# Attention scores of a Pre-LN block with a mixture of experts: PSUM tiles of two banks in place of one

## The chip, the cores and the metric

The kernel runs on one core of a Trainium2 chip. The metric is the device time of one execution in microseconds (us). The time before is 618.14 us, the median of three runs (616.91, 624.91 and 618.14).

## The reference

One transformer block over x of shape 8 x 512 x 128, everything in float32: layer norm, causal attention with 16 heads of width 8, a residual sum, a second layer norm, and 8 experts of width 512, of which each token uses the two that its gate likes best.

```
x = x + attn(layernorm(x))          # q, k, v of 16 heads x 8; scores causal; softmax; @ Wo + bo
x = x + ffn(layernorm(x))           # 8 experts, top 2 by softmax(x @ gate_w.T), relu, weighted sum
```

## The kernel before, in words

The work is laid out by batch (b, 8 of them), and inside a batch by groups of four heads (g, 4 per batch). Every engine has a fixed order of instructions. It is written by hand as several generators ("lanes"): each yields the point of the schedule, counted in batches, at which its next piece is to stand, and the lane with the smallest point goes next. The lanes that matter here:

- `project` (L393) makes layer norm, q and k of a batch ahead of time, splits them into three bf16 parts and sends them through DRAM into the packed buffers q2 and k2, where a head's three parts lie on the rows of one matmul.
- `shifts` (L555) finds each query's largest score. For each pair of heads it goes through three units (`S_UNITS`): TensorE writes blocks of scores into PSUM tiles named s (L593, L598), and VectorE takes a maximum over each tile into pm (L612). After two pairs it reduces pm to nm, splits it into two bf16 parts (L618 to L629), transposes them on TensorE, copies them on ScalarE (L562) and sends them by two DMAs on SyncE's queue (POOL's for batch 0) into two rows of q2 (L568). So a later matmul subtracts the maximum by itself. The transpose and the DMAs are popped from a list, one entry after each unit. This lane runs 0.55 of a batch (`LEAD`) ahead of the next.
- `attend` (L638) computes the scores once more, transposed and with the maximum subtracted, into PSUM tiles named st (L740, L745). ScalarE takes the exponential of each into pt (L750). TensorE multiplies pt with v into po (`product`, L657, matmuls at L667). Every unit ends with `go_on` (L645), which pops one waiting product and one late step (the division at L682, the transpose of the output, the projection).
- `route`, `dispatch` and `experts` run beside the attention of later batches: gate, choice, scatter of the tokens to DRAM, tiles of 128 tokens per expert (ph at L1238, the relu at L1245 or L1247, py at L1097), a store, and a weighted sum at the end (`sums`). POOL's scatters and stores also wait for the last exponential ahead of them (`in_order`). About 490 us into the span the attention is over and only expert work is left.

PSUM has 8 banks of 512 float32 columns. One, ps_o, holds po; three, ps_mm, serve everything else; four, the pool ps_sc, serve s and st in rotation, one bank per tile, and the ph of the late expert tiles. Which free buffer of a pool a tile gets is settled when the program is built.

A unit names, for each bank, the heads and blocks that lie in it. The first and second units of a pair fill two banks (one bank per head), the third fills one bank with blocks of both heads. So a group of four heads has ten s banks and ten st banks, each with its own maximum (L612) or its own exponential (L750) over 512 columns. Nothing needs a bank's neighbour: the maximum over one bank can run while TensorE fills the next.

In the program's order an s unit and an st unit alternate: s unit, st unit with a product or a late step behind it, s unit, and so on; in a group there are six of each.

Of the kernel before, what the change touches and what calls it, by code (L numbers as in the profile page):

```python
# [9 lines left out]
F32 = mybir.dt.float32  # L10
# [8 lines left out]
P = 128  # L19
# [7 lines left out]
def preln_attn_moe(ctx: ExitStack, tc: tile.TileContext, x, wq, wk, wv, wo, bo,  # L27
# [52 lines left out]
    WARM = (40, 75, 4)  # L80
    XB = 3

    S_UNITS = (
        (((0, 3, 0),), ((1, 3, 0),)),
        (((0, 0, 0), (0, 2, P)), ((1, 0, 0), (1, 2, P))),
        (((0, 1, 0), (1, 1, 2 * P)),),
    )
    T_UNITS = (
        (((0, 0, 0),), ((1, 0, 0),)),
        (((0, 1, 0), (0, 3, 3 * P)), ((1, 1, 0), (1, 3, 3 * P))),  # L90
        (((0, 2, 0), (1, 2, 2 * P)),),
    )


    GROUPS = ((0, 1, 2, 3, 4, 5, 6), (7,))
# [24 lines left out]
    work = ctx.enter_context(tc.tile_pool(name="work", bufs=2))  # L120
    small = ctx.enter_context(tc.tile_pool(name="small", bufs=2))
    slots = ctx.enter_context(tc.tile_pool(name="slots", bufs=1, space=DRAM))
    ps_sc = ctx.enter_context(tc.tile_pool(name="ps_sc", bufs=4, space=PSUM))
    ps_mm = ctx.enter_context(tc.tile_pool(name="ps_mm", bufs=3, space=PSUM))
    ps_o = ctx.enter_context(tc.tile_pool(name="ps_o", bufs=1, space=PSUM))

# [428 lines left out]
    def shifts():  # L555
# [18 lines left out]
        for b in range(B):  # L574
            for g in range(G):
                t0 = b - LEAD + g / G + (0.1 if b == 0 < g else 0.0)
                yield t0
                assert b in packed
                q2, k2 = q2_buf[b % 2], k2_buf[b % 2]

                pm = pm_buf[g % 2].rearrange("p (n u) t k -> p u n (t k)", u=2)
                for pr in range(2):
                    n = 2 * g + pr
                    for i, unit in enumerate(S_UNITS):
                        yield t0 + (3 * pr + i) / 24
                        for v, bank in enumerate(unit):
                            ps = ps_sc.tile(
                                [P, T], F32, tag="sc", name=f"s_{b}_{n}_{i}_{v}"
                            )
                            for u, t, at in bank:  # L590
                                h, q = 2 * n + u, ts(t, P)
                                if t > 0:
                                    nc.tensor.matmul(  # L593
                                        ps[:, at : at + t * P], lhsT=q2[:KS, h, q],
                                        rhs=k2[:KS, h, : t * P],
                                        start=(at == 0), stop=True, skip_group_check=True,
                                    )
                                nc.tensor.matmul(  # L598
                                    ps[:, at + t * P : at + (t + 1) * P],
                                    lhsT=q2[:, h, q], rhs=k2[:, h, q],  # L600
                                    start=(at + t == 0), stop=True, skip_group_check=True,
                                )
                            blocks = ps.rearrange("p (a q) -> p a q", q=P)
                            if i == 0:
                                top, src = pm[:, v, pr, 12:13], ps
                            elif i == 1:
                                top, src = pm[:, v, pr, 3:7], blocks
                            else:
                                top, src = pm[:, :, pr, 8], ps.rearrange(
                                    "p (u k) -> p u k", u=2  # L610
                                )
                            nc.vector.tensor_reduce(top, src, AX.X, ALU.max)  # L612
                        if t0 + (3 * pr + i) / 24 < 0:
                            keep_warm(WARM[2], f"{g}_{pr}_{i}")
                        if late:
                            late.pop(0)()
                nm = small.tile([P, HG * NT], F32, tag="nm", name=f"nm_{b}_{g}")
                nc.vector.tensor_reduce(  # L618
                    nm, pm_buf[g % 2].rearrange("p h t k -> p (h t) k"), AX.X, ALU.max,
                    negate=True,  # L620
                )
                nh = nh_buf[g % 2]
                nm = nm.rearrange("p (h o a) -> p h o a", o=2, a=2)
                hi, lo = (
                    nh[:, ts(l, HG * NT)].rearrange("p (h a o) -> p h o a", a=2, o=2)
                    for l in range(2)
                )
                V.tensor_copy(hi, nm)
                V.tensor_tensor(lo, nm, hi, ALU.subtract)  # L629
                if b > 0:  # L630
                    late.append(lambda: None)
                late.append(lambda b=b, g=g, nh=nh: transposed(b, g, nh))
# [5 lines left out]
    def attend():  # L638
# [11 lines left out]
            for step in ready:  # L650
                step()

        def at_cols(pt, unit, u, at, W):
            v = u if len(unit) == 2 else 0
            return pt[:, v, at : at + W]

        def product(b, g, pts, unit, first, last):  # L657
            va = va_buf[b % 2]
            for j in sorted({j for bank in unit for _, j, _ in bank}):
                W = T - j * P  # L660
                for pr in range(2):
                    for bank in unit:
                        for u, i, at in bank:
                            if i != j:
                                continue
                            h = 2 * pr + u
                            nc.tensor.matmul(  # L667
                                po[32 * h : 32 * h + VC, j * P :],
                                lhsT=va[:, j, HG * g + h, :],
                                rhs=at_cols(pts[pr], unit, u, at, W),  # L670
                                start=(first and j == 0), stop=(last and j == 2),
                            )
            if last:
                ob = work.tile([P, T], F32, tag="ob", name=f"ob_{b}_{g}", bufs=1)
                nc.scalar.copy(ob, po)
                if b < B - 1:
                    late.append(lambda: None)
                late.append(lambda: divide(b, ob, g))
                if g == G - 1:
                    added.add(b)  # L680
# [40 lines left out]
        for b in range(B):  # L721
            for g in range(G):
                yield b + g / G
                assert (b, g, 2) in shifted
                q2, k2 = q2_buf[b % 2], k2_buf[b % 2]
                for i, unit in enumerate(T_UNITS):
                    pts = []
                    for pr in range(2):
                        yield b + g / G + (2 * i + pr + 0.5) / 24
                        n = 2 * g + pr  # L730
                        pt = work.tile(
                            [P, 2, T], F32, tag="pt", name=f"pt_{b}_{n}_{i}", bufs=6
                        )
                        for v, bank in enumerate(unit):
                            ps = ps_sc.tile(
                                [P, T], F32, tag="sc", name=f"st_{b}_{n}_{i}_{v}"
                            )
                            for u, j, at in bank:
                                h, k = 2 * n + u, ts(j, P)
                                nc.tensor.matmul(  # L740
                                    ps[:, at : at + P], lhsT=k2[:, h, k], rhs=q2[:, h, k],
                                    start=(at == 0), stop=True, skip_group_check=True,
                                )
                                if j < NT - 1:
                                    nc.tensor.matmul(  # L745
                                        ps[:, at + P : at + T - j * P],
                                        lhsT=k2[:KO, h, k], rhs=q2[:KO, h, (j + 1) * P :],
                                        start=False, stop=True, skip_group_check=True,
                                    )
                            last_exp[0] = nc.scalar.activation(pt[:, v, :], ps, AF.Exp, scale=SCALE)  # L750
                        pts.append(pt)
                        go_on()
                    products.append(lambda b=b, g=g, pts=pts, unit=unit, i=i: product(
                        b, g, pts, unit, i == 0, i == 2))
                attended.add((b, g))
        t = B
        while products or late:
            t += 0.5 / 24
            yield t
            go_on()  # L760

# [272 lines left out]
    def experts():  # L1034
# [192 lines left out]
        for n, (s, i) in enumerate(tiles):  # L1227
            first, m = quad(s, i)
            yield when(s, i + 1)
            if after(s, i):  # L1230
                ph = ps_sc.tile([P, T], F32, tag="sc", name=f"ph_{s}_{i}")
                hT = work.tile([P, 2, T], F32, tag="pt", name=f"hT_{s}_{i}", bufs=6)
                hT = hT[:, 0, :].rearrange("p (c t) -> p c t", c=FC)
            else:
# [140 lines left out]
```

## Time and profile before

| | |
|---|---|
| median of three runs | 618.14 us |
| the profiled execution, its own time | 610.58 us |
| its span from first to last instruction | 608.9 us |
| mean granted clock of TensorE | 0.949 |
| VectorE: maximum over 128x512 (L612) | 320 of 683 ns, 206.4 us |
| ScalarE: exponential over 128x512 (L750) | 320 of 599 ns, 177.6 us |
| attention of batch 1, 4, 6 (from its first st to the next batch's) | 49.2, 58.0, 56.3 us |

In the page, each engine has a line with its busy time; a busy TensorE is not one at its peak, since the ends of matmuls are modelled. In the groups, a row shows line, engine, operation and tiles, the count, the busy time with the mean of one, and the idle time of the engine just before such instructions with the one that ended it. In the timeline each row has its start in us, its length, engine, line and what it writes from what; brackets hold the idle time before it.

### The profile page before, as it was taken

What the parts mean: (1) busy time and instruction counts of PE and PEld (TensorE: products, weight loads), DVE (VectorE), ACT (ScalarE), POOL (GpSimd) and SP (SyncE); (2) the same over time, 40 slices, a digit from 0 to 9 for tenths busy, and PEclk for the clock granted to TensorE, in tenths of its full rate; (3) what the DMA queues carried; (4) which work ended last, traced back from release to release, by engine and by line L of the source; (5) the groups of instructions that cost most, each with busy time, mean ns of one, the idle gap of its engine ahead of it and who ended that gap; (6) DMA issues with size and microseconds to landing.
All of it is one profiled execution on the core that took longest, in us unless ns stands there. A gap on an engine that the chain in (4) does not pass through costs nothing.

```text
span 608.9 us, 14141 instructions
## 1 busy us (share of the span) xinstructions
PE 526.4 (86%) x4804; PEld 381.0 (63%) x4804; DVE 435.1 (71%) x1407; ACT 312.2 (51%) x685; POOL 188.4 (31%) x220
## 2 busy tenths in 40 slices
PE   7879998988877888889899999998999889889980
PEld 4655455555444554656566677775667579789970
DVE  6787688678986777787888786898684256323594
ACT  2646566655564574546455565564464434244530
POOL 3032200203413230162243213514314534655441
PEclk9989799999987899999899999999899999899995
DMA  2658187286379436521662486232135588667793
GB/s 56 177 135 169 44 215 164 67 186 169 80 152 166 116 96 166 135 60 44 156 145 60 119 173 170 71 87 88 49 81 145 163 252 234 181 196 240 218 315 111
DMA packets 68762, 86.07 MB, mean 141 GB/s; under 512 B 11540, under 2 KB 50748, under 8 KB 66652
## 3 DMA queue, kind: packets, MB, share of 16 engines
q1 hardware_dynamic: 63300, 75.10, 49.0%
q0 software_dynamic: 4800, 9.41, 4.6%
q8 instruction: 39, 0.64, 0.5%
q10 hardware_dynamic: 592, 0.66, 0.3%
q14 instruction: 31, 0.25, 0.2%
HBM read 61.34 MB, written 26.16 MB: 144 GB/s over the span
## 4 chain that ended last, share of the span: by engine, by line
PE 48%; DVE 24%; ACT 9%; DMA 7%; issue 7%; SPq 2%; another core or an unknown queue 1%; POOL 1%; ACTq 0%; DVEq 0%; POOLq 0%
DVE pm L612 11%; PE po L667 10%; PE py L1097 7%; PE ph L1238 6%; ACT pt L750 5%; PE st L745 4%; PE s L593 4%; PE st L740 4%; PE s L598 3%; PE oqp L687 3%; DMA q<-nmT 2%; DMA q<-ys 2%; PE pq L444 2%; DVE x L1316 2%; ACT hT L1245 2%
## 5 line engine op out<-in xcount | busy, mean ns | idle before, releaser
L750 ACT ACTIVATE pt<-st 128x512 f32<-128x512 f32 x320 | 177.6, 599 | 133.3 <-PE st L740 55.5
L612 DVE TENSOR_REDUCE pm<-s 128x1 f32<-128x512 f32 (+2 forms) x320 | 206.4, 683 | 31.2 <-PE s L598 25.7
L1135 POOL DMA_INDIRECT ys<-yo,to x78 | 75.5, 968 | 139.3 <-ACT pt L750 21.6
L593 PE MATMUL s<-k,q 72*128 72x384 bf16 (+2 forms) x384 | 94.6, 282 | 19.5 <-DVE pm L612 9.2
L740 PE MATMUL st<-q,k 128*128 128x128 bf16 x512 | 94.0, 225 | 12.6 <-DMA q<-nmT 4.6
L598 PE MATMUL s<-k,q 128*128 128x128 bf16 x512 | 94.9, 225 | 7.3 <-ACT pt L750 4.9
L667 PE MATMUL po<-pt,va 128*9 128x512 f32 (+3 forms) x1024 | 99.5, 460 | 1.1 <-ACT pt L750 1.0
L1003 POOL DMA_INDIRECT xs<-xn_f,slot x64 | 62.2, 972 | 116.8 <-ACT pt L750 85.1
L745 PE MATMUL st<-q,k 74*128 74x256 bf16 (+2 forms) x384 | 94.6, 284 | 0.0
L1097 PE MATMUL py<-w_sb,hT 128*128 x624 | 87.1, 281 | 7.7 <-issue 4.5
L1097 PEld LDWEIGHTS py<-w_sb,hT 128*128 128x128 f32 x624 | 77.7, 194 | 10.0 <-issue 5.5
L598 PEld LDWEIGHTS <-q 128*128 128x128 bf16 x512 | 51.6, 101 | 30.9 <-issue 27.8
L593 PEld LDWEIGHTS <-q 72*128 72x128 bf16 x384 | 38.2, 101 | 37.7 <-issue 31.3
L740 PEld LDWEIGHTS <-k 128*128 128x128 bf16 x512 | 52.5, 103 | 12.1 <-issue 5.2
L745 PEld LDWEIGHTS <-k 74*128 74x128 bf16 x384 | 38.4, 100 | 19.6 <-issue 14.3
L667 PEld LDWEIGHTS po<-pt,va 128*9 128x9 f32 x1024 | 21.3, 90 | 35.5 <-issue 24.0
L1238 PE MATMUL ph<-xgT,wt 128*128 128x128 f32 x288 | 40.1, 282 | 0.7 <-ACT xgT L1199 0.6
L1238 PEld LDWEIGHTS ph<-xgT,wt 128*128 128x128 f32 x288 | 35.0, 192 | 5.4 <-PE st L740 1.7
L1245 ACT ACTIVATE hT<-ph,q 128x128 f32<-128x128 f32 x72 | 20.9, 371 | 27.9 <-PE ph L1238 14.8
L690 DVE RECIPROCAL rd<-oqp 128x16 f32<-128x16 f32 x32 | 8.2, 255 | 36.9 <-PE oqp L687 31.6
L687 PEld LDWEIGHTS oqp<-ident,ob 128*128 128x128 f32 x128 | 14.4, 148 | 29.7 <-issue 28.3
L454 POOL TENSOR_TENSOR part<-rest,part 128x512 bf16<-128x512 f32 x14 | 16.1, 1158 | 50.0 <-ACT part L453 21.8
(170 smaller groups left out, 717.2 us busy)
## 6 DMA issues: line engine op xcount, KB each, us to landing
wt<-wrows SPq DMA_DIRECT2D x36, 322.0 KB
k<-kparts SPq DMA_DIRECT2D x42, 192.0 KB
q<-wrows SPq DMA_DIRECT2D x24, 322.0 KB
k<-wrows SPq DMA_DIRECT2D x18, 322.0 KB
q<-qparts SPq DMA_DIRECT2D x30, 192.0 KB
q<-ys SPq DMA_DIRECT2D x15, 256.0 KB
k<-xs SPq DMA_DIRECT2D x42, 65.0 KB
qparts<-part SPq DMA_DIRECT2D x14, 192.0 KB
```

The lines of the kernel that those rows point to most:

```text
L593: nc.tensor.matmul(ps[:, at : at + t * P], lhsT=q2[:KS, h, q], rhs=k2[:KS, h, : t * P], start=(at == 0), stop=True, skip_group_check=True,)
L598: nc.tensor.matmul(ps[:, at + t * P : at + (t + 1) * P], lhsT=q2[:, h, q], rhs=k2[:, h, q], start=(at + t == 0), stop=True, skip_group_che ...
L612: nc.vector.tensor_reduce(top, src, AX.X, ALU.max)
L667: nc.tensor.matmul(po[32 * h : 32 * h + VC, j * P :], lhsT=va[:, j, HG * g + h, :], rhs=at_cols(pts[pr], unit, u, at, W), start=(first and ...
L740: nc.tensor.matmul(ps[:, at : at + P], lhsT=k2[:, h, k], rhs=q2[:, h, k], start=(at == 0), stop=True, skip_group_check=True,)
L745: nc.tensor.matmul(ps[:, at + P : at + T - j * P], lhsT=k2[:KO, h, k], rhs=q2[:KO, h, (j + 1) * P :], start=False, stop=True, skip_group_c ...
L750: last_exp[0] = nc.scalar.activation(pt[:, v, :], ps, AF.Exp, scale=SCALE)
L1003: ins = nc.gpsimd.indirect_dma_start(out=xs[k], out_offset=bass.IndirectOffsetOnAxis(ap=slot[b][:, j * NT + i : j * NT + i + 1], axis=0), ...
L1097: nc.tensor.matmul(py, lhsT=hT[:, c, :], rhs=w2_sb[:, bass.ds(at[s, i] + c * E * D, D)], start=(c == 0), stop=(c == FC - 1),)
L1135: ins = nc.gpsimd.indirect_dma_start(out=ys[k], out_offset=bass.IndirectOffsetOnAxis(ap=to[s, first][:, i - first : i - first + 1], axis=0 ...
L1238: nc.tensor.matmul(ph[:, ts(c, P)], lhsT=wt[s, i][:, ts(c, P)], rhs=turned[s, first][:, ts(i - first, P)], start=True, stop=True,)
L1245: nc.scalar.activation(hT[:, c, :], ph[:, ts(c, P)], AF.Relu, bias=bias)
```

## The change

The pool ps_sc gets two buffers of two banks (1024 columns) in place of four of one. The units are drawn anew, for a group of four heads at once: five s units and five st units, each of which fills both banks of one tile. One maximum (L612 before) reads all 1024 columns, and so does one exponential (L750 before). The matmuls into the tiles are the same ones; their number, shapes and sums do not change. The points of the schedule within a group go in steps of 1/20 of a batch in place of 1/24, so lists that pop one entry per unit pop five per group in place of six. A product is queued after the second, the fourth and the fifth st unit. The late ph tiles take half of a two-bank tile each, in turn.

```diff
     S_UNITS = (
-        (((0, 3, 0),), ((1, 3, 0),)),
-        (((0, 0, 0), (0, 2, P)), ((1, 0, 0), (1, 2, P))),
-        (((0, 1, 0), (1, 1, 2 * P)),),
+        (((0, 0, 3, 0),), ((0, 1, 3, 0),)),
+        (((0, 0, 0, 0), (0, 0, 2, P)), ((0, 1, 0, 0), (0, 1, 2, P))),
+        (((1, 0, 3, 0),), ((1, 1, 3, 0),)),
+        (((1, 0, 0, 0), (1, 0, 2, P)), ((1, 1, 0, 0), (1, 1, 2, P))),
+        (((0, 0, 1, 0), (0, 1, 1, 2 * P)), ((1, 0, 1, 0), (1, 1, 1, 2 * P))),
     )
     T_UNITS = (
-        (((0, 0, 0),), ((1, 0, 0),)),
-        (((0, 1, 0), (0, 3, 3 * P)), ((1, 1, 0), (1, 3, 3 * P))),
-        (((0, 2, 0), (1, 2, 2 * P)),),
+        (((0, 0, 0, 0),), ((0, 1, 0, 0),)),
+        (((1, 0, 0, 0),), ((1, 1, 0, 0),)),
+        (((0, 0, 1, 0), (0, 0, 3, 3 * P)), ((0, 1, 1, 0), (0, 1, 3, 3 * P))),
+        (((1, 0, 1, 0), (1, 0, 3, 3 * P)), ((1, 1, 1, 0), (1, 1, 3, 3 * P))),
+        (((0, 0, 2, 0), (0, 1, 2, 2 * P)), ((1, 0, 2, 0), (1, 1, 2, 2 * P))),
     )
+    UNITS = len(S_UNITS)
...
-    ps_sc = ctx.enter_context(tc.tile_pool(name="ps_sc", bufs=4, space=PSUM))
+    ps_sc = ctx.enter_context(tc.tile_pool(name="ps_sc", bufs=2, space=PSUM))
...
-                pm = pm_buf[g % 2].rearrange("p (n u) t k -> p u n (t k)", u=2)
-                for pr in range(2):
-                    n = 2 * g + pr
-                    for i, unit in enumerate(S_UNITS):
-                        yield t0 + (3 * pr + i) / 24
-                        for v, bank in enumerate(unit):
-                            ps = ps_sc.tile(
-                                [P, T], F32, tag="sc", name=f"s_{b}_{n}_{i}_{v}"
+                pm = pm_buf[g % 2].rearrange("p (n u) t k -> p n u (t k)", u=2)
+                for i, unit in enumerate(S_UNITS):
+                    yield t0 + i / (UNITS * G)
+                    ps = ps_sc.tile([P, 2, T], F32, tag="sc", name=f"s_{b}_{g}_{i}")
+                    for v, bank in enumerate(unit):
...
-                            if i == 0:
-                                top, src = pm[:, v, pr, 12:13], ps
-                            elif i == 1:
-                                top, src = pm[:, v, pr, 3:7], blocks
-                            else:
-                                top, src = pm[:, :, pr, 8], ps.rearrange(
-                                    "p (u k) -> p u k", u=2
-                                )
-                            nc.vector.tensor_reduce(top, src, AX.X, ALU.max)
...
+                    pr, _, t, _ = unit[0][0]
+                    if t == 3:
+                        top, src = pm[:, pr, :, 12], ps
+                    elif t == 0:
+                        top, src = pm[:, pr, :, 3:7], ps.rearrange("p v (a q) -> p v a q", q=P)
+                    else:
+                        top, src = pm[:, :, :, 8], ps.rearrange("p v (u k) -> p v u k", u=2)
+                    nc.vector.tensor_reduce(top, src, AX.X, ALU.max)
...
+                pts = []
                 for i, unit in enumerate(T_UNITS):
-                    pts = []
-                    for pr in range(2):
-                        yield b + g / G + (2 * i + pr + 0.5) / 24
...
+                    yield b + g / G + (i + 0.5) / (UNITS * G)
+                    pt = work.tile([P, 2, T], F32, tag="pt", name=f"pt_{b}_{g}_{i}", bufs=6)
+                    ps = ps_sc.tile([P, 2, T], F32, tag="sc", name=f"st_{b}_{g}_{i}")
...
-                            last_exp[0] = nc.scalar.activation(pt[:, v, :], ps, AF.Exp, scale=SCALE)
-                        pts.append(pt)
-                        go_on()
-                    products.append(lambda b=b, g=g, pts=pts, unit=unit, i=i: product(
-                        b, g, pts, unit, i == 0, i == 2))
...
+                    last_exp[0] = nc.scalar.activation(pt, ps, AF.Exp, scale=SCALE)
+                    pts.append((pt, unit))
+                    go_on()
+                    if i % 2 == 1 or i == UNITS - 1:
+                        products.append(lambda b=b, g=g, pts=pts, i=i: product(
+                            b, g, pts, i == 1, i == UNITS - 1))
+                        pts = []
...
-                ph = ps_sc.tile([P, T], F32, tag="sc", name=f"ph_{s}_{i}")
+                if sum(after(*a) for a in tiles[:n]) % 2 == 0:
+                    two = ps_sc.tile([P, 2, T], F32, tag="sc", name=f"ph_{s}_{i}")
+                    ph = two[:, 0, :]
+                else:
+                    ph = two[:, 1, :]
```

## The prediction

> **What bounds the kernel now.** I read the page first (busy time, chain, groups), then busy time by stretches, then the timeline of one stretch.
>
> ```profile
> PE 526.4 (86%) x4804; PEld 381.0 (63%) x4804; DVE 435.1 (71%) x1407; ACT 312.2 (51%) x685; POOL 188.4 (31%) x220
> ...
> PE 48%; DVE 24%; ACT 9%; DMA 7%; issue 7%; SPq 2%; another core or an unknown queue 1%; POOL 1%; ACTq 0%; DVEq 0%; POOLq 0%
> DVE pm L612 11%; PE po L667 10%; PE py L1097 7%; PE ph L1238 6%; ACT pt L750 5%; PE st L745 4%; PE s L593 4%; PE st L740 4%; PE s L598 3%; PE oqp L687 3%; DMA q<-nmT 2%; DMA q<-ys 2%; PE pq L444 2%; DVE x L1316 2%; ACT hT L1245 2%
> ...
> L750 ACT ACTIVATE pt<-st 128x512 f32<-128x512 f32 x320 | 177.6, 599 | 133.3 <-PE st L740 55.5
> L612 DVE TENSOR_REDUCE pm<-s 128x1 f32<-128x512 f32 (+2 forms) x320 | 206.4, 683 | 31.2 <-PE s L598 25.7
> L593 PE MATMUL s<-k,q 72*128 72x384 bf16 (+2 forms) x384 | 94.6, 282 | 19.5 <-DVE pm L612 9.2
> ```
>
> TensorE carries the chain for half the span, VectorE for a quarter; ScalarE is half idle. The largest single entry of the chain is the maximum. The last row shows that TensorE's score matmuls already wait for it.
>
> ```profile
> 100.00:160.00 60.00, 51.21 (x487) 31.38 (x486) 49.49 (x143) 35.17 (x69) 14.20 (x14) 0.97 0.58 142
> 340.00:400.00 60.00, 58.01 (x579) 42.83 (x578) 45.79 (x145) 33.53 (x77) 19.52 (x20) 1.00 0.56 138
> ```
>
> The columns are length, then busy time of PE, PEld, DVE, ACT and POOL, the granted clock, DMA share and GB/s. In early batches VectorE (49.5 of 60) and TensorE share the load; once expert tiles run, TensorE is full (58.0 of 60), so what holds TensorE back costs time there.
>
> ```profile
> 206.81 0.22 PE L740 MATMUL st<-q,k 128*128 128x128 bf16 x1
> 206.87 0.22 PE L745 MATMUL st<-q,k 74*128 74x128 bf16 x1
> ...
> 207.04 0.22 PE L598 MATMUL s<-k,q 128*128 128x128 bf16 x1
> ...
> 207.40 1.28 DVE L612 TENSOR_REDUCE pm<-s 128x1 f32<-128x512 f32 x2
> ...
> 209.02 1.25 DVE L612 TENSOR_REDUCE pm<-s 128x4 f32<-128x512 f32 x2
> ...
> 211.09 0.69 DVE L612 TENSOR_REDUCE pm<-s 128x2 f32<-128x512 f32 x1
> ...
> 211.83 0.32 PE L593 MATMUL s<-k,q 72*128 72x384 bf16 x1 [0.68 <-DVE pm L612]
> ...
> 212.22 0.28 PE L740 MATMUL st<-q,k 128*128 128x128 bf16 x2
> 212.33 0.27 PE L745 MATMUL st<-q,k 74*128 74x256 bf16 x1
> 212.44 0.22 PE L740 MATMUL st<-q,k 128*128 128x128 bf16 x1
> 212.53 1.08 ACT L750 ACTIVATE pt<-st 128x512 f32<-128x512 f32 x2 [0.65 <-PE st L740]
> ```
>
> At 207.04 TensorE begins the next s unit although the maxima over the last one run only from 207.40 to 208.68: the four banks let it run ahead. At 211.83 it can't, and idles 0.68 us until the maximum of 211.09 ends. At 212.53 the exponential starts on its first bank while the second is being filled (the last matmul starts at 212.44).
>
> **The change part by part.** The sum is made against the profiled execution: 610.58 us (span 608.9, 1.7 around it). The median of the runs is 7.6 above it; I add that at the end.
>
> Durations. A 128-column bf16 matmul follows the last after 0.056 us (206.81 to 206.87). 1024 columns of scores are eight such, 0.45 us at most. A reader starts 0.03 us after the modelled end of the last matmul (212.28 + 0.22 = 212.50, read at 212.53), so 0.21 us after TensorE is free to go on. The waiting matmul starts 0.05 us after the read ends (211.78 to 211.83). Two maxima in a row take 1.28 us, one 0.684, so a second 512 columns costs 0.60 in a separate instruction. The short reduction over 64 columns (L618) takes 0.220 us: (684 - 220)/448 is 1.036 ns a column. One maximum over 1024 thus takes 0.684 + 0.53 = 1.22 us. For ScalarE, the bf16 copy over 2048 columns (L248) takes 1893 ns and the exponential over 512 takes 599: 0.842 ns a column, so 599 + 431 = 1.03 us against 1.086 for two.
>
> 1. VectorE's saving. 128 pairs save 0.06 each (8 us); 32 times two lone maxima (1.37) become one (1.22) (5 us): 13 us of 206. The maximum is on the chain for 65 of its 206 us, 31%: -4 us. Bounds: 0 and -13.
>
> [...]
>
> 2. ScalarE's saving by the same count: 128 x 0.06 + 32 x (1.20 - 1.03) = 13 us; 30 of its 178 us are on the chain, 17%: -2 us. Bounds: 0 and -13.
>
> 3. TensorE's waits. With two tiles, a fill must wait until the whole tile is read: 0.21 + 1.22 + 0.05 = 1.48 us after an s fill, 0.21 + 1.03 + 0.05 = 1.29 after an st fill. The instruction order of the changed program says which tile each fill takes and what TensorE has to do since that tile's last fill. Example (batch 4, group 2): s_2, st_1 (0.44 of work), s_3: 1.04 us short. I counted this for all 318 fills with row durations (0.22 for a 128x128 float32 product, 0.87, 0.66, 0.44 and 0.23 for four heads' po at 512 to 128 columns). 58 s fills after s are short, by 32 us in all; 35 st after st, 22 us; 24 s fills that take the tile of the st fill just before, 18 us; 13 st after s, 7 us: together 79 us. The same count for before, by bank, a unit's longer wait alone, gives 44 us. The rows of before name only about 30 us of such waits of TensorE (9.2 for L593 on the maximum, and L598, L740 and the waits on exponentials beside it), 0.68 of the count, since one wait shortens the next. So (79 - 44) x 0.68 = +24 us. Bounds: where only TensorE-led stretches count (69%), +16. From above: in the trace 109 s fills start before the maxima over the s unit ahead have ended, by 82 us together, and 45 st fills by 20 us; if all of that is lost in TensorE-led stretches, 102 x 0.69 = +70. I take +24, since it is counted on the order that will run. Behind a waiting fill stand, on TensorE's queue, the st fill, the product and the expert matmuls; ScalarE and POOL's stores wait for those.
>
> 4. VectorE's waits. Where VectorE is the limit, an s fill can start only after its maximum ends: 0.05 + 0.45 + 0.21 = 0.7 us until the next can start. Before, the second bank's maximum covered that. Now other VectorE work must: in the changed order 22 pairs of maxima have nothing between them, 43 have less than 0.7; the shortfall is 24 us in all. Times 31%: +7 us. Bounds: 0 (TensorE leads anyway) and +24.
>
> 5. The rows of the maximum. The transposed maximum's two DMAs go out after the third of five units in place of the third of six; the copy, the transpose and the two DMAs on SyncE's queue each come later by 2/20 + 1/4 - (2/24 + 1/4) = 1/60 batch, 0.9 us of 56. Three st fills waited for them (4.6 us in all): +3 us. Bounds: 0 and, if the issue at 184 us (8.7 us to landing) repeats twice, +12.
>
> 6. At nothing: division, output transpose and projection come at fifths in place of sixths of a group (expert or attention matmuls cover them; without cover about 0.6 us for each of 8 batches). The late ph tiles: a tile waits for the relu of three tiles ago in place of four, and these tiles come about 2 us apart (py and ph 0.95 us each), against a relu of 0.37; the last 120 us stay.
>
> Sum: -4 - 2 + 24 + 7 + 3 = +28 us: 610.6 + 28 = 638.6 us profiled, 646 as a median.
>
> **The rivals.** (a) Same within 2%: waits 3 and 4 fall where something else (POOL, DMA, the other engine) would have stopped the fills. For it: TensorE's streaming, about 476 us by the same durations, leaves 130 us of slack. Against: 58.0 of 60 busy from 340 us. With term 3 at its lower end less the savings: 16 - 6 = +10, about 628 us.
> (b) Backlog: VectorE's queue is late (the median s bank is read 0.68 us after its fill), so each fill waits longer than my prompt reader. Term 3 at its upper end and 4 half: 70 + 12 - 6 + 3 = +79, 697 us. Against: what holds TensorE back lets VectorE catch up; half of it, 665 to 680, is likelier.
> (c) Faster: VectorE is the limit everywhere and other work covers the 0.7 us between maxima, as at 95 to 109 us, where it is hardly ever idle. Then the 13 us come in full: 605 us. The point is at about 0.7 us of other VectorE work between two maxima; 94 of 159 gaps have it, 65 don't, and TensorE leads late. So it is unlikely.
>
> **How the numbers follow.** Forecast (633 to 663 us) 0.50; (a) 0.25; (b) 0.16; (c) 0.09. What can be told from no change is about 2%, 12.4 us: below 605.8 faster, above 630.5 slower. Faster holds most of (c), 0.08. Same holds (a) and the rest of (c) less a little beyond 630.5: 0.24. Slower 0.68. The range leaves out (c) and the upper part of (b): 614 to 684. The forecast's own range is 633 to 663.
>
> **What would show it.** Right: one maximum near 1.22 us and one exponential near 1.03, 160 each; L593 and L598 idle longer before them, released by the maximum and the exponential (30 us grows to 50 or more); batches 4 to 6 longer than 56 to 58 us, the last 120 us unchanged. Wrong: batches 4 to 6 at the old length (a), DMA q<-nmT growing on the chain, or maxima over 1.28 us.

## The result and the profile after

The changed kernel takes 640.38 us (median of 4 runs, 636.5 to 645.97), the kernel before beside it on the same chip 619.99 us (4 runs, 616.91 to 624.91): a ratio of 1.039, interval 1.033 to 1.044. It is slower. Ratios and intervals, here and below, are taken over the fast executions alone, so a ratio can differ from the quotient of the medians beside it (1.033 here). The profiled execution took 645.97 us with a span of 644.3 (before 608.9), at a mean granted clock of 0.924 (before 0.949).

The page of the changed kernel, busy time by engine and four groups (busy us, mean ns of one, idle time just before them and what ended most of it):

```profile
PE 529.7 (82%) x4800; PEld 385.8 (60%) x4800; DVE 428.3 (66%) x1247; ACT 302.4 (47%) x525; POOL 187.5 (29%) x220
...
L613 DVE TENSOR_REDUCE pm<-s 128x8 f32<-128x1024 f32 (+2 forms) x160 | 194.7, 1219 | 60.5 <-PE s L601 56.0
L736 ACT ACTIVATE pt<-st 128x1024 f32<-128x1024 f32 x160 | 164.2, 1026 | 143.3 <-PE st L731 65.0
L596 PE MATMUL s<-k,q 72*128 72x256 bf16 (+2 forms) x384 | 91.1, 287 | 31.3 <-DVE pm L613 17.2
L601 PE MATMUL s<-k,q 128*128 128x128 bf16 x512 | 90.7, 228 | 20.2 <-DVE pm L613 14.6
```

VectorE is 6.8 us less busy than before (435.1 to 428.3) and ScalarE 9.8 us less (312.2 to 302.4). The idle time ahead of the maxima doubled, 31.2 to 60.5 us, and that ahead of the first row of the s matmuls went from 19.5 to 31.3.

The list of waits of the changed kernel (us in total, times, longest), TensorE's on the readers of the scores:

```profile
PE s L596 <- DVE pm L613: 17.2, 20, 2.9
PE s L601 <- DVE pm L613: 14.6, 16, 2.5
PE s L596 <- ACT pt L736: 10.7, 11, 1.7
PE s L601 <- ACT pt L736: 5.4, 9, 1.4
PE st L726 <- ACT pt L736: 3.1, 7, 0.7
PE st L726 <- DVE pm L613: 1.3, 3, 0.5
```

The same six entries of the kernel before:

```profile
PE s L593 <- DVE pm L612: 9.2, 12, 2.0
PE s L598 <- DVE pm L612: 1.8, 4, 1.0
PE s L593 <- ACT pt L750: 8.3, 14, 2.3
PE s L598 <- ACT pt L750: 4.9, 9, 0.8
PE st L740 <- ACT pt L750: 3.1, 7, 0.7
PE st L740 <- DVE pm L612: 2.9, 13, 0.4
```

Together they are 52.3 us now and 30.2 before. All of the growth is on s: on maxima 11.0 to 31.8, on exponentials 13.2 to 16.1. The waits of st went from 6.0 to 4.4.

One place shows how such a wait comes about, and what follows it. The timeline of the changed kernel from 162.2 us (start, length, engine and line, idle time before it):

```profile
162.19 0.22 PE L601 MATMUL s<-k,q 128*128 128x128 bf16 x1
...
163.72 0.69 DVE L709 TENSOR_TENSOR x<-pp,x 128x512 f32<-128x512 f32 x1 [2.69 <-PE po L661]
...
165.10 1.22 DVE L613 TENSOR_REDUCE pm<-s 128x8 f32<-128x1024 f32 x1
166.37 0.32 PE L596 MATMUL s<-k,q 72*128 72x384 bf16 x1 [2.91 <-DVE pm L613]
...
167.92 1.22 DVE L613 TENSOR_REDUCE pm<-s 128x2 f32<-128x1024 f32 x1
169.19 0.27 PE L601 MATMUL s<-k,q 128*128 128x128 bf16 x1 [1.77 <-DVE pm L613]
```

The maximum ends at 166.32 and the matmul starts at 166.37, 0.05 later: the fill waited for the read of both banks. Of the 2.91 us, 1.22 is the read itself; most of the rest is other VectorE work ahead of it, L709 first. That lateness is one of order as much as of load: VectorE has a fixed order, L709 stands ahead of the maximum, and VectorE sat idle for 2.69 us until L709 could start, although the last matmul into the tile (the one of 162.19) had ended 1.3 us before. TensorE waits again 2.8 us later, for 1.77 us, once more behind other VectorE work. The same stretch in steps of 1 us (length; busy us of PE, PEld, DVE, ACT, POOL; granted clock, DMA share, GB/s):

```profile
164.00:165.00 1.00, 0.00 (x0) 0.00 (x0) 0.93 (x4) 1.00 (x3) 0.00 (x0) 1.00 0.00 0
165.00:166.00 1.00, 0.00 (x0) 0.00 (x0) 1.00 (x2) 0.46 (x1) 0.00 (x0) 1.00 0.04 6
166.00:167.00 1.00, 0.63 (x6) 0.46 (x6) 0.97 (x5) 0.00 (x0) 0.00 (x0) 1.00 0.09 4
167.00:168.00 1.00, 0.42 (x4) 0.16 (x2) 0.93 (x6) 0.55 (x1) 0.00 (x0) 1.00 0.09 18
168.00:169.00 1.00, 0.00 (x0) 0.00 (x0) 1.00 (x2) 0.48 (x1) 0.00 (x0) 0.50 0.40 115
...
173.00:174.00 1.00, 1.00 (x6) 1.00 (x6) 0.03 (x1) 0.00 (x0) 0.83 (x1) 0.50 0.20 68
174.00:175.00 1.00, 1.00 (x10) 0.94 (x9) 0.77 (x3) 0.18 (x1) 0.13 (x1) 0.59 0.20 67
175.00:176.00 1.00, 1.00 (x13) 0.83 (x11) 0.64 (x1) 0.54 (x2) 0.00 (x0) 1.00 0.00 0
```

TensorE is idle in the first two of these microseconds and again from 168; its clock is halved from 168 to 174.8 us.

Where the time went, by the parts of the profiled span: from the start to the last copy of attention products 487.5 us before and 507.9 after (+20.4); from there to the end 121.4 and 136.4 (+15.0). Of the attention part, the first batches lost most: batch 0 went from 46.3 to 52.0 us, batch 2 from 53.9 to 62.1, batch 4 from 58.0 to 61.1; batches 5 and 6 from 56.7 to 58.7 and from 56.3 to 56.9; the last batch became shorter, from 66.4 to 62.5. In two stretches that the prediction showed of before:

```profile
100.00:160.00 60.00, 49.75 (x480) 31.60 (x483) 44.28 (x114) 30.84 (x43) 9.17 (x9) 0.91 0.55 133
340.00:400.00 60.00, 55.46 (x553) 40.34 (x555) 44.59 (x117) 31.95 (x52) 16.84 (x17) 0.97 0.54 130
```

The early one has VectorE 5.2 us less busy (49.49 to 44.28), 29 instructions fewer, and the granted clock is 0.91 for 0.97. The late one has TensorE at 55.5 for 58.0. Neither engine is full any more; the waits above, of each for the other, grew.

The last part grew because of the late ph tiles. The changed kernel's timeline there:

```profile
548.98 0.88 ACT L1237 ACTIVATE hT<-ph,k 128x128 f32<-128x128 f32 x3 [4.69 <-issue]
549.90 0.35 DVE L1239 TENSOR_SCALAR hT<-ph,k 128x128 f32<-128x128 f32 x1 [3.53 <-ACT hT L1237]
...
550.31 2.08 PE L1230 MATMUL ph<-xgT,k 128*128 128x128 f32 x8 [3.82 <-DVE hT L1239]
```

The next products start 0.06 us after the last relu of the ph before (549.90 + 0.35). Of the 42 late ph tiles, 21 sit in the second half of a tile whose first half is the ph before, and the tile is released as a whole. The list of waits has 15.7 us (15 times) of L1230 on that relu. The wait shown is the longest and not typical: most of its 3.82 us comes from ScalarE, which began its relus only after 4.69 us in which it waited for nothing that the profile shows. The other 14 waits take 11.9 us together.

### The profile page after: what moved, and what is told of

Same layout as the page of the kernel before. It is cut to its first block, busy times and chain, and to the rows that moved or that the text cites. A ratio compares the mean times of both kernels' runs of the same rounds, so it can differ in the third digit from the quotient of the medians.

```text
span 644.3 us, 13751 instructions
## 1 busy us (share of the span) xinstructions
PE 529.7 (82%) x4800; PEld 385.8 (60%) x4800; DVE 428.3 (66%) x1247; ACT 302.4 (47%) x525; POOL 187.5 (29%) x220
## 5 line engine op out<-in xcount | busy, mean ns | idle before, releaser
L613 DVE TENSOR_REDUCE pm<-s 128x8 f32<-128x1024 f32 (+2 forms) x160 | 194.7, 1219 | 60.5 <-PE s L601 56.0
L736 ACT ACTIVATE pt<-st 128x1024 f32<-128x1024 f32 x160 | 164.2, 1026 | 143.3 <-PE st L731 65.0
L596 PE MATMUL s<-k,q 72*128 72x256 bf16 (+2 forms) x384 | 91.1, 287 | 31.3 <-DVE pm L613 17.2
L601 PE MATMUL s<-k,q 128*128 128x128 bf16 x512 | 90.7, 228 | 20.2 <-DVE pm L613 14.6
L726 PE MATMUL st<-q,k 128*128 128x128 bf16 x512 | 89.6, 226 | 11.2 <-DMA q<-nmT 4.7
L661 PE MATMUL po<-pt,va 128*9 128x512 f32 (+3 forms) x1024 | 97.1, 475 | 0.0
L991 POOL DMA_INDIRECT xs<-xn_f,slot x64 | 62.1, 970 | 105.5 <-ACT pt L736 60.9
L731 PE MATMUL st<-q,k 74*128 74x256 bf16 (+2 forms) x384 | 90.6, 286 | 0.0
L1085 PEld LDWEIGHTS py<-w_sb,hT 128*128 128x128 f32 x624 | 80.2, 201 | 1.2 <-issue 0.4
L596 PEld LDWEIGHTS <-q 72*128 72x128 bf16 x384 | 39.1, 102 | 54.3 <-issue 46.3
L1230 PE MATMUL ph<-xgT,wt 128*128 128x128 f32 x288 | 40.2, 283 | 1.7 <-ACT xgT L1187 1.5
L1230 PEld LDWEIGHTS ph<-xgT,wt 128*128 128x128 f32 x288 | 35.4, 192 | 8.1 <-ACT xgT L1187 2.5
L1230 PE MATMUL ph<-xgT,q 128*128 128x128 f32 x192 | 28.4, 294 | 10.0 <-DVE hT L1239 9.7
L1230 PEld LDWEIGHTS ph<-xgT,q 128*128 128x128 f32 x192 | 25.0, 203 | 13.0 <-DVE hT L1239 11.4
```

Source lines behind the costliest of these rows:

```text
L596: nc.tensor.matmul(ps[:, v, at : at + t * P], lhsT=q2[:KS, h, q], rhs=k2[:KS, h, : t * P], start=(at == 0), stop=True, skip_group_check=True,)
L601: nc.tensor.matmul(ps[:, v, at + t * P : at + (t + 1) * P], lhsT=q2[:, h, q], rhs=k2[:, h, q], start=(at + t == 0), stop=True, skip_group_ ...
L661: nc.tensor.matmul(po[32 * h : 32 * h + VC, j * P :], lhsT=va[:, j, HG * g + h, :], rhs=p, start=(first and j == 0), stop=(last and j == 2),)
L726: nc.tensor.matmul(ps[:, v, at : at + P], lhsT=k2[:, h, k], rhs=q2[:, h, k], start=(at == 0), stop=True, skip_group_check=True,)
L731: nc.tensor.matmul(ps[:, v, at + P : at + T - j * P], lhsT=k2[:KO, h, k], rhs=q2[:KO, h, (j + 1) * P :], start=False, stop=True, skip_grou ...
L736: last_exp[0] = nc.scalar.activation(pt, ps, AF.Exp, scale=SCALE)
```

## The experiments

What was in question: the theory was that fills wait because a tile of two banks is free only when both are read (term 3 of the prediction). Rivals: the order of five units alone costs the time; the shared ph tiles cost it; the long instruction itself costs it, because its reader ends later; or what is missing is not the early release of a bank but the number of buffers that can pass between s and st. The runs were made in several sittings, and the kernel before took between 594.94 and 619.99 us in them, so ratios are compared, each to the kernel before beside it on the same chip. "Attention" and "rest" are the two parts of the profiled span as above.

| run | median us | ratio | interval | attention / rest |
|---|---|---|---|---|
| e1 ph in a tile of its own | 612.16 | 1.027 | 1.018–1.036 | 495.8 / 111.9 |
| e2 five units, tiles of one bank | 603.39 | 1.008 | 1.003–1.014 | 477.2 / 113.5 |
| e3 only s in wide tiles | 624.21 | 1.045 | 1.037–1.053 | 507.7 / 115.2 |
| e4 only st in wide tiles | 614.78 | 1.024 | 1.014–1.035 | 498.8 / 113.5 |
| e5 the change again | 623.18 | 1.048 | 1.041–1.055 | 499.5 / 123.7 |
| e6 e1 again | 612.37 | 1.032 | 1.025–1.039 | 494.1 / 112.8 |
| e7 e1 with two reads a tile | 623.98 | 1.051 | 1.044–1.058 | 507.1 / 112.2 |
| e8 e2 with split pools | 612.64 | 1.029 | 1.020–1.038 | 500.4 / 115.1 |
| e9 before, five banks | 629.09 | 1.016 | 1.007–1.025 | 498.1 / 126.1 |
| e10 before, three banks | 662.3 | 1.058 | 1.045–1.071 | not known |
| e11 e4, s with three banks | 638.04 | 1.024 | 1.009–1.039 | 506.8 / 128 |
| e12 e1 with split pools | 648.11 | 1.052 | 1.037–1.068 | 523.9 / 123.0 |

**e1: each late ph in a tile of its own.**

```diff
-                if sum(after(*a) for a in tiles[:n]) % 2 == 0:
-                    two = ps_sc.tile([P, 2, T], F32, tag="sc", name=f"ph_{s}_{i}")
-                    ph = two[:, 0, :]
-                else:
-                    ph = two[:, 1, :]
+                ph = ps_sc.tile([P, 2, T], F32, tag="sc", name=f"ph_{s}_{i}")[:, 0, :]
```

> The changed kernel, but each late ph takes a two-bank tile of its own (half of it unused), in place of sharing one with its neighbour. Theory A: the last stretch grew from 121 to 136 us because the first matmul of every second late ph waits for the relu of the ph beside it in the same tile; then the last stretch falls back to 119 to 125 us and the time to 625 to 631 us, with the stretch up to the end of attention as in the changed kernel (508 us). Rival: the last stretch is longer because transfers or the granted clock differ; then it stays at 133 to 139 and the time at 636 to 644.

Measured: 1.027, or about 636 us at the speed of the first chip, above the 625 to 631 that theory A gave and at the edge of the rival's 636 to 644. Whether this is less than the change had to be seen on the same chip, in e5 and e6.

**e2: the changed order with tiles of one bank, four in rotation** (a maximum and an exponential for each bank, ph as before).

```diff
-    ps_sc = ctx.enter_context(tc.tile_pool(name="ps_sc", bufs=2, space=PSUM))
+    ps_sc = ctx.enter_context(tc.tile_pool(name="ps_sc", bufs=4, space=PSUM))
...
-                    ps = ps_sc.tile([P, 2, T], F32, tag="sc", name=f"s_{b}_{g}_{i}")
                     for v, bank in enumerate(unit):
+                        ps = ps_sc.tile([P, T], F32, tag="sc", name=f"s_{b}_{g}_{i}_{v}")
...
-                    last_exp[0] = nc.scalar.activation(pt, ps, AF.Exp, scale=SCALE)
+                        last_exp[0] = nc.scalar.activation(pt[:, v, :], ps, AF.Exp, scale=SCALE)
```

> Tiles of one bank, four in rotation, with a maximum or an exponential of 512 columns each, as in the kernel before; but the five units a group, the steps of 1/20, the products and late steps as in the changed kernel. Theory A (the tiles cost it: a fill must wait for a whole tile's read, and late ph share a tile): 612 to 624 us, attention over at 485 to 492. Rival B (the new units and their schedule cost it: late steps, products and the maximum's rows stand later): 632 to 644 us, attention over at 500 to 508.

Measured: 1.008, interval 1.003 to 1.014. Theory A's range held. The order of five units costs something under 1.5%, and the figure is rough: ten runs spread from 592.52 to 613.26 us. Most of the loss is in the tiles. Its waits:

```profile
PE s L601 <- DVE pm L613: 8.9, 16, 2.5
PE s L596 <- DVE pm L613: 8.7, 19, 0.8
```

17.6 us against 31.8 of the change, in the same order.

**e3 and e4: only s, or only st, in tiles of two banks**, the other side in two tiles of one bank (the late ph uses the pool of one-bank tiles).

```diff
+    ps_s = ctx.enter_context(tc.tile_pool(name="ps_s", bufs=1, space=PSUM))
...
-                    ps = ps_sc.tile([P, 2, T], F32, tag="sc", name=f"s_{b}_{g}_{i}")
+                    ps = ps_s.tile([P, 2, T], F32, tag="sc", name=f"s_{b}_{g}_{i}")
...
-                    ps = ps_sc.tile([P, 2, T], F32, tag="sc", name=f"st_{b}_{g}_{i}")
+                        ps = ps_sc.tile([P, T], F32, tag="sc", name=f"st_{b}_{g}_{i}_{v}")
```

> Only the s side keeps a two-bank tile and one maximum of 1024 columns (a pool of one such tile); the st side has two one-bank tiles and exponentials of 512, and the late ph take these one-bank tiles. Theory A with the larger share on the maximum (term 3: 32 of 79 us of shortfall after s alone, 22 after st alone; VectorE's wait of term 4 is here too): 626 to 636 us. Rival (the exponential's side is what costs): 614 to 622 us.

> The mirror: only the st side keeps a two-bank tile and one exponential of 1024 columns; the s side has two one-bank tiles and maxima of 512, and the late ph take these. Theory A with the larger share on the maximum: 616 to 626 us, below the run with the wide maximum. Rival (the exponential's side is what costs): 628 to 640 us.

Measured: 1.045 with wide s, 1.024 with wide st, or about 647 and 634 us at the speed of the first chip. Wide s costs more, as theory A has it, but both are above its ranges. And both kernels also fix two banks to each side, where the change lets any tile go to either. So neither figure is the price of a wide tile until that is measured alone: e8.

**e5 and e6: the change, and e1, again on one chip.** e5 is the changed kernel unaltered, e6 is e1 unaltered.

> The changed kernel as it is, beside the next three on one chip, so that its ratio to the kernel before can be set against theirs. Expected by all theories: 1.033 to 1.044 times the kernel before.

> The changed kernel with a tile of its own for each late ph, again beside the others: 1.020 to 1.033 if the neighbour's relu cost the last stretch some 7 us; the same ratio as the changed kernel (1.033 to 1.044) if that was the chip.

Measured: 623.18 and 612.37 us, 10.8 us (1.7%) apart, with intervals of the ratios that do not meet. The rest of the span is 123.7 and 112.8 us, 10.9 apart, as much as the medians. (The two profiled executions differ by 16.3 us; the other 5.4 lie in the attention, where the two kernels are alike, at granted clocks of 0.933 and 0.954.) The waits of ph on the relu in e5,

```profile
PE ph L1230 <- DVE hT L1239: 10.8, 15, 1.8
```

and in e6:

```profile
PE ph L1226 <- DVE hT L1235: 1.1, 1, 1.1
```

So the shared tile costs 1.7%, and it is shown.

**e7: e6 with two reads of one bank after both fills**, one wait ahead and one release behind them, 160 instructions more on each engine.

```diff
-                    nc.vector.tensor_reduce(top, src, AX.X, ALU.max)
+                    for v, bank in enumerate(unit):
...
+                        nc.vector.tensor_reduce(top, src, AX.X, ALU.max)
...
-                    last_exp[0] = nc.scalar.activation(pt, ps, AF.Exp, scale=SCALE)
+                    for v in range(2):
+                        last_exp[0] = nc.scalar.activation(pt[:, v, :], ps[:, v, :], AF.Exp, scale=SCALE)
```

> The same with two maxima and two exponentials of 512 columns a tile in place of one of 1024. The tile, the one wait ahead of the reads and the one release behind them stay, so only the longer instructions are undone (13 us of VectorE, 13 us of ScalarE by terms 1 and 2, 6 us of them on the chain by my sum). Theory A (the length of the instruction saves a little, the tile's release costs): 0.5 to 1.5% above the run with own ph tiles, 1.030 to 1.050. Rival (the long instruction itself is what costs, since a reader holds its engine for 1.2 us at a time): equal or below, 1.010 to 1.027.

Measured: 1.051 against e6's 1.032 on the same chip, 11.6 us more: 1.9%, where theory A gave 0.5 to 1.5%. The maxima of e7's page:

```profile
L614 DVE TENSOR_REDUCE pm<-s 128x4 f32<-128x512 f32 (+2 forms) x320 | 205.0, 684 | 54.8 <-PE s L601 54.4
```

e6 has 160 of 1220 ns, 194.8 us together: 10.2 us less, and as much idle time ahead of them. ScalarE's exponentials take 174.0 in e7 and 164.0 in e6. So the long instruction is a gain, about what one of the two engines saves in busy time (10.2 and 10.0 us), and not the cause of the loss.

**e8: e2 with the four banks split, two for s and two for st and ph.**

```diff
-    ps_sc = ctx.enter_context(tc.tile_pool(name="ps_sc", bufs=4, space=PSUM))
+    ps_sc = ctx.enter_context(tc.tile_pool(name="ps_sc", bufs=2, space=PSUM))
+    ps_s = ctx.enter_context(tc.tile_pool(name="ps_s", bufs=2, space=PSUM))
...
-                        ps = ps_sc.tile([P, T], F32, tag="sc", name=f"s_{b}_{g}_{i}_{v}")
+                        ps = ps_s.tile([P, T], F32, tag="sc", name=f"s_{b}_{g}_{i}_{v}")
```

> One-bank tiles and reads of 512 columns with five units a group, but two banks for s alone and two for st alone, in place of four for both. It is the control for the runs in which one side alone had a wide tile. Theory A (what costs is that a bank can't be refilled until its neighbour is read too): 1.005 to 1.018, near the run with four shared banks. Rival (what costs is that each side is left with two banks, whatever a tile's size): 1.022 to 1.045, as the runs with one wide side.

Measured: 1.029, where e2 had 1.008. Its waits for the maximum:

```profile
PE s L597 <- DVE pm L614: 23.0, 52, 1.4
PE s L602 <- DVE pm L614: 15.0, 32, 2.5
```

38.0 us with every bank released by itself, more than the change has. The rival's range held, and theory A's did not: a bank's own release is not enough. Two banks for s that can't borrow are as bad as two wide tiles that can. With e8 as the base, and net of what the long instruction saves, wide st costs nothing that can be told (e4: 1.024 against 1.029) and wide s about 1.6% (e3: 1.045).

**e9 and e10: the kernel before with five and with three banks for scores**; the pool for the other products gives or takes the bank.

```diff
-    ps_sc = ctx.enter_context(tc.tile_pool(name="ps_sc", bufs=4, space=PSUM))
-    ps_mm = ctx.enter_context(tc.tile_pool(name="ps_mm", bufs=3, space=PSUM))
+    ps_sc = ctx.enter_context(tc.tile_pool(name="ps_sc", bufs=5, space=PSUM))
+    ps_mm = ctx.enter_context(tc.tile_pool(name="ps_mm", bufs=2, space=PSUM))
```

> The kernel before with five one-bank score tiles in rotation in place of four, and two in place of three banks for everything else (ps_mm). Theory C (scores are held by how many banks can be refilled on their own: four shared banks 1.008, two and two 1.029, two wide tiles 1.03): below the kernel before, 0.97 to 0.995, if two banks are enough for the rest. Rival (four are enough; the loss came from the wide tile's release alone): 0.998 to 1.02, since the rest has one bank less.

> The kernel before with three one-bank score tiles and four banks for the rest. Theory C: slower, 1.02 to 1.05, as with two and two. Rival: 0.99 to 1.01.

Measured: 1.016 with five, interval 1.007 to 1.025, and 1.058 with three (e10 has 3 and 4 in place of 5 and 2). Three banks cost at least as much as the change does, and a little more than theory C gave. With five, theory C's gain did not come, and the rival's range held. But that kernel also has one bank less for everything else, and both its attention (498.1 us) and its rest (126.1) are longer than those of the kernel before on the first chip (487.5 and 121.4): what the fifth bank alone is worth is not told apart.

**e11: e4 with three banks for s**, again with two for the other products.

```diff
-    ps_s = ctx.enter_context(tc.tile_pool(name="ps_s", bufs=2, space=PSUM))
+    ps_s = ctx.enter_context(tc.tile_pool(name="ps_s", bufs=3, space=PSUM))
...
-    ps_mm = ctx.enter_context(tc.tile_pool(name="ps_mm", bufs=3, space=PSUM))
+    ps_mm = ctx.enter_context(tc.tile_pool(name="ps_mm", bufs=2, space=PSUM))
```

> Only the st side has a two-bank tile and one exponential of 1024 columns; the s side has three one-bank tiles and maxima of 512 columns (late ph too), and ps_mm two banks. Theory C: the third bank for the maxima brings this below the run with two (1.024): 1.000 to 1.015. Rival (the wide exponential is what cost there): 1.02 to 1.03.

Measured: 1.024 with an interval of 1.009 to 1.039, the same as e4 and in the rival's range, not in theory C's. But ps_mm has a bank less here too, so for the same reason as e9 it does not decide between the two.

**e12: e1 with one wide tile for s and one for st**, ph taking the two in turn.

```diff
-    ps_sc = ctx.enter_context(tc.tile_pool(name="ps_sc", bufs=2, space=PSUM))
+    ps_sc = ctx.enter_context(tc.tile_pool(name="ps_sc", bufs=1, space=PSUM))
+    ps_s = ctx.enter_context(tc.tile_pool(name="ps_s", bufs=1, space=PSUM))
...
-                    ps = ps_sc.tile([P, 2, T], F32, tag="sc", name=f"s_{b}_{g}_{i}")
+                    ps = ps_s.tile([P, 2, T], F32, tag="sc", name=f"s_{b}_{g}_{i}")
...
-                ph = ps_sc.tile([P, 2, T], F32, tag="sc", name=f"ph_{s}_{i}")[:, 0, :]
+                pool = (ps_sc, ps_s)[sum(after(*a) for a in tiles[:n]) % 2]
+                ph = pool.tile([P, 2, T], F32, tag="sc", name=f"ph_{s}_{i}")[:, 0, :]
```

> Two-bank tiles with one read of 1024 columns, each late ph with a tile to itself, but one tile fixed for s and one for st, in place of two for both. With shared tiles the s fills waited some 15 us for the exponential of the st unit just before them (its tile was taken when that looked sooner than the maximum); here those waits must be gone, and the waits on the maximum grow. Theory C (sharing lets a side borrow): 1.040 to 1.055, against 1.027 to 1.032 shared. Rival (borrowing a tile that has just been filled is itself the loss): 1.010 to 1.025.

Measured: 1.052, interval 1.037 to 1.068, against 1.027 and 1.032 for e1 and e6, which differ from it in the split alone (the late ph take both pools). So tiles of two banks still borrow from one another, and it is worth about 2%, as it is with tiles of one bank (e8 against e2). Waits of s for the maximum are 61.6 us in e12 (37.3 and 24.3).

Put together, from e2 (1.008): splitting the pools 2% (e8); making the tiles wide with the pools split another 2.3% (e12 against e8). Making them wide with the pool shared, about 2% (e1 and e6 against e2). This last is net of the 1.9% that the long instructions save (e7). So handling two banks as one tile, whose reads wait for both fills and whose refill waits for both reads, costs about 4% (e7 against e2); which of the two waits costs the more was not tried. The shared ph tile adds 1.7%. Each of these differences is uncertain by about a point. None of the kernels beats the kernel before.

## Why the prediction was right, and where it was not

**Side and size.** 646 us were predicted, 1.045 times the median shown; measured was 1.039, and 1.048 in e5. But that is partly luck: two errors cancelled. Without the shared ph tiles the change costs 1.027 to 1.032 (e1, e6), 16 to 19 us and not 28; the tail, which was put at nothing, brought the missing 10.

**Term 3, TensorE's waits (+24).** The rows grew by 22 us (30.2 to 52.3). In pieces the working was not right: s after s was counted at 32 us and came at 31.8, but in 36 waits where 58 were counted, so each was longer; s on the st tile just before at 18 and came at 16.1; both without the factor of 0.68; st after st and st after s were counted at 22 and 7 and came at 3.1 and 1.3. The likely reason, not tried by itself, is that an st fill stands behind an s fill that has waited already, so that the wait is paid once. The count added both, and the factor happened to make up for it.

**Terms 1 and 2, the savings (-4 and -2).** The durations were right: 1219 ns against 1.22 us, 1026 against 1.03. The worth was too small: the two reads of e7 cost 11.6 us, nearly twice the 6. The share of the chain was too small a factor; a likely reason, not tried, is that the read's length also sits in each wait of a fill for a whole tile. In place of -6 the sum would have -11.6, and with term 3 at 22 it would give 22 + 7 - 11.6 + 3 = +20, near the 16 to 19 of e1 and e6. e6 and e7 show 10.2 us of VectorE for 160 maxima more, 64 ns each. Breaking up the instruction paid here only with the tile broken up too: e7 breaks up the instruction alone and loses (1.051 against e6's 1.032), e2 breaks up the tile as well and is at 1.008.

**Term 4, VectorE's waits (+7).** The idle time of the maxima on s grew by 30 us (25.7 to 56.0), where the shortfall was counted at 24. Its price can't be read off the changed kernel, whose chain of waits breaks off near its end. e6 differs in the late ph alone, and its chain is whole; shares of the span by engine:

```profile
PE 53%; DVE 19%; DMA 13%; ACT 6%; issue 4%; SPq 3%; POOL 2%; ACTq 0%; POOLq 0%; DVEq 0%
```

TensorE had 48% before and VectorE 24%; the maxima fell from 10.7% to 8.3% of the span (65 to 50 us). VectorE carries less of the chain than before, so the 31% that the step multiplied by is not confirmed. The stretches don't settle it: batch 2, which lies partly where the two engines share the load (51.2 and 49.5 of 60 at 100 to 160 us), lost 8.2 us, but batch 0, where TensorE leads (51.1 of 55 against VectorE's 41.8 at 45 to 100 us), lost 5.7; the batches of 4 to 6, where TensorE leads too (157.6 of 171 against VectorE's 139.4 at 250 to 421 us), lost 3.1, 2.0 and 0.6. "Batches 4 to 6 longer" came true, but by little; the loss lies earlier than the prediction put it.

**Term 5, rows of the maximum (+3).** The waits for that transfer are 4.6 us of the st matmuls and 2.7 of their weight loads before, 4.7 and 6.8 after; the two may count the same time. On the chain the transfer has 2.1% of the span before (13 us), 3.9% in e6 (24 us): 11 us more, inside the term's bounds but above its value. e2, which has the later rows and no wide tiles, is at 1.008 in all (5 us) with 2.9%. The term was rather too small, and was not measured alone. The prediction named growth of this transfer on the chain as a sign of being wrong, and it did grow.

**Term 6, the last 120 us unchanged (0).** This step failed. The working took three tiles of rotation and a relu of 0.37 us and asked whether a tile would be free in time. It missed that two neighbouring ph now are one tile, so that a ph waits for the relu of the ph just before it. e5 and e6 show 10.9 us in the rest of the span.

**The rivals.** (a) fell: the waits are real. (c) fell, though the saving it rests on is there (e7). (b) was not reached: the waits grew by 22 us and not by 70. But its mechanism, a reader that is late because VectorE has other work, is what 163.7 us shows. Its likelier half, "665 to 680", is not half of 79 us: that gives 658, inside the forecast's own range. The fault in the theory behind term 3 is e8's: release by bank alone did not bring the time back (1.029, where e2 has 1.008). What the kernel before has is four buffers that are refilled one at a time by whichever side needs them; the change halves that number. The number alone is not the whole of it: three banks (e10, 1.058) cost more, in the order of six units, than two wide tiles do in that of five (e1 and e6).

**Open.** How much of the loss on the first chip is the waits themselves and how much the lower clock; which wait of a whole tile costs the more, that of its reads or that of its refill; why the order of five units alone costs 0.8%; what a fifth bank would bring without taking one elsewhere, since every kernel here already divides eight banks among its pools.

## What to carry to other kernels

Count accumulator buffers by how many can be refilled independently, and not only by their bytes: with the bytes unchanged, joining two banks under one instruction saved 10 us of busy time on each reader here (10.2 and 10.0, e6 against e7) and cost more in fills that stood still (about 4% of the time, for 1.9% saved). Sharing one pool among two users was worth 2%, with narrow (e8 against e2) and with wide tiles (e12 against e1 and e6) alike. When a buffer is made wider, look at every other user of its pool: two ph put into one wide tile here were chained to each other (10.8 us of waits in e5 for 1.1 in e6, and 1.7% of the time), though they never touch the same bytes.

## What was not expected of the hardware

The mean granted clock is lower in the slower kernel (0.924 for 0.949), and in the stretch shown above it falls after two short waits. In its steps of 1 us it is 1.00 or 0.50, with a mixed value (0.59) only in the step that holds the rise, and the halved stretch from 168 to 174.8 us begins after 2.91 us without a matmul and inside a second idle stretch of 1.77. Over the whole span 538 of 608 such steps before are at 1.00 and 49 at 0.50, and 532 and 78 of 644 after; the other 21 and 34 stand one at a time at an edge of a halved stretch. So the mean clock gives the time at half speed: (1 - 0.949) x 2 x 608.9 = 62 us before and (1 - 0.924) x 2 x 644.3 = 98 us after. At 0.50 a 128-column bf16 matmul of scores is followed by the next after 0.11 us (169.89 to 170.00), at 1.00 after 0.06 (166.75 to 166.81). If TensorE was never idle in the 36 us more, they cost 18 us of work, an upper estimate of the clock's part of the 35 us by which the span grew. The four runs of the changed kernel go the same way: 645.97 us at 0.924, 641.13 at 0.929, 639.63 at 0.934, 636.5 at 0.938. Which is the cause and which the effect no run here separates. But most of the loss is there at an equal clock too, in single executions. On the chip of e5 and e6 the kernel before took 592.41 us at 0.952 and 592.54 at 0.956, and e6 608.7 at 0.954, 16 us more; it took 598.04 at 0.944, and the change (e5) 622.23 at 0.944, 24 us more. Just ahead of the fall TensorE was busy for 0.63 us from 166 to 167 and for 0.42 from 167 to 168; how much idleness brings the fall about, no run here shows.
